# The FFN pair's fifth product: one VectorE add to the partial sum, and a GpSimd add to one result instead of two

## The chip, the core and the metric

The kernel runs on one core of one Trainium2 chip. The metric is the device time of one execution in microseconds (us). Every engine of the core has its own instruction stream and runs it in order: TensorE (PE, matrix products; PEld is its weight load, which overlaps), VectorE (DVE), ScalarE (ACT), GpSimd (POOL), and SyncE (SP), which here only issues transfers. Engines wait for each other through semaphores.

## What is computed

The reference is one transformer block with modulated layer norms, for 8 batches of 1024 rows by 256 columns, in float32. Cut to what matters:

```python
mod = (silu(c) @ wmod).reshape(8, 6, 1, 256)
sa, ca, ga, sb, cb, gb = (mod[:, i] for i in range(6))
# ga and gb are then pushed away from zero
h = layernorm(x) * (1 + ca) + sa
x = x + ga * softmax((h * w_lhs) @ (h * w_rhs).T) @ h
h = layernorm(x) * (1 + cb) + sb
x = x + gb * (relu(h @ W1 + b1) @ W2 + b2)
```

The change lies in `relu(h @ W1 + b1)`, where h has 256 columns and W1 has 1024.

## The kernel before

**Stages.** The attention of batch b runs row block by row block (8 blocks i of 128 rows). While the attention of batch b runs, the FFN of batch b-1 (the rows in two halves g of 512) is worked off beside it: steps i = 0, 1 and i = 4, 5 compute the first FFN product of a half, steps 2, 3 and 6, 7 the second. Batch 7's FFN has nothing beside it and closes the kernel. In each step PE also makes scores (`direct`, L412), turns row maxima (`max_turn`, L468), and multiplies the exponentials with the values (`product` L501, `pair_begin` L549, `pair_end` L593). DVE takes row maxima (`row_max`, L463), subtracts them (`subtract`, L475), transposes score blocks (`mirror`, L435) and closes attention blocks (`pair_out`, L608 to L621). ACT copies scores (L419) and does the exponentials (L484).

**Order.** The order of the calls in the step loop (L1150 on) is the order of the instructions on each engine: `pin` at the end ties each instruction to the one before it on its engine. So nothing overtakes anything; an instruction that comes later or takes longer moves all that stands behind it on its engine, until that engine would have idled anyway.

**The pair.** The first FFN product is made with seven half-size products instead of eight (Strassen's method in Winograd's form). For chunk c of 128 hidden columns and its partner c + 4, with the 512 rows as two halves lo and hi of 256, the seven products go to three PSUM tiles:

- `pair_products` (L728): PE writes P1 and P5 to `pa` (lo, hi), two more to `pb`, two more to `pc`. ACT copies `pa` to `kept` in SBUF (L747), so `kept[:, hi]` is the fifth product.
- `pair_sums` (L756): DVE makes the partial sum `u` = pb.lo + bias + P1 (L762), then `far` = pb.hi + bias step + u, which goes to f[c+4].hi (L765), then f[c].lo (L768), and f[c+4].lo = pc.hi + far (L771).
- `pair_last` (L773): PE writes the seventh product over `pa`.lo; DVE makes f[c].hi = pa.lo + u (L779); then one GpSimd instruction (L780) adds the fifth product to f[c].hi and f[c+4].hi together, 2 x 256 columns.
- `pair_relu` (L787): ACT applies relu to f[c] (L789) and f[c+4] (L790), 512 columns each.
- `pair_turn` (L794): GpSimd makes sums and differences of the four blocks for the second FFN product (L799 to L802).

There are 8 batches x 2 halves x 4 chunks = 64 pairs. Below they are numbered k = 0 to 63 in order: step i = 0 of batch 1 has k = 0 and 1, step 1 has 2 and 3, step 4 has 4 and 5, step 5 has 6 and 7, and batch 2 goes on with 8. k = 56 to 63 are the closing FFN.

**Buffers.** `pa`, `pb`, `pc` and most other PSUM tiles of PE (`po`, `pp`, `pq`, `pr`, and the second product's `ya` to `yd`) share a pool of four buffers, tag "a". PE's first write to a new tile waits until the last reader of the buffer's old tile is done; a buffer is given again in the order in which buffers came free. So within a step the second pair's `pb` takes the buffer that the first pair's `pb` left (last read by L765), its `pc` that of the first `pc` (last read by L771), and the tile after it (`po` or `pp`) that of the first `pa` (last read by L779). `u` and `kept` have two buffers each in SBUF.

**The step i = 4 to 5**, on DVE, in order: sums of the first pair (L762 to L771), the transposes of `y_turn` (L867) and of `mirror` (L435), L779 of the first pair, a small L277 of the next batch's norm (ACT's L281 waits for it), sums and L779 of the second pair, then the transposes of `prepare_blocks` (L322, which wait for ACT's L281), L475, L463, `pair_out` (L608 to L621), and then step 5's first pair.

Of the kernel before, what the change touches and what calls it, by code (L numbers as in the profile page):

```python
# [13 lines left out]
ALU = mybir.AluOpType  # L14
# [3 lines left out]
P = 128  # L18
# [6 lines left out]
def adaln_block_kernel(  # L25
# [13 lines left out]
    nc = tc.nc  # L39
# [7 lines left out]
    H2 = HALF // 2  # L47
    NH = NI // 2
# [673 lines left out]
    lo, hi = slice(0, H2), slice(H2, HALF)  # L722
    pairs = {}

    def mm(out, lhsT, rhs):
        nc.tensor.matmul(out, lhsT=lhsT, rhs=rhs, start=True, stop=True)  # L726
# [29 lines left out]
    def pair_sums(b, g, c):  # L756
        pa, pb, pc, kept = pairs[c]
        f = ffn["f"]
        u = work.tile([P, H2], F32, tag="u", name=f"u_{b}_{g}_{c}", bufs=2)
        pairs[c] = pa, kept, u  # L760
        far = f[:, c + NH, hi]
        nc.vector.scalar_tensor_tensor(  # L762
            u, pb[:, lo], b1_col(c), kept[:, lo], ALU.add, ALU.add
        )
        nc.vector.scalar_tensor_tensor(  # L765
            far, pb[:, hi], b1_step[:, c : c + 1], u, ALU.add, ALU.add
        )
        nc.vector.scalar_tensor_tensor(  # L768
            f[:, c, lo], pc[:, lo], b1_col(c), kept[:, lo], ALU.add, ALU.add
        )  # L770
        nc.vector.tensor_tensor(f[:, c + NH, lo], pc[:, hi], far, ALU.add)  # L771

    def pair_last(b, g, c):  # L773


        pa, kept, u = pairs.pop(c)
        f = ffn["f"]
        mm(pa[:, lo], w1s[:, 2, ts(c, P)], ffn["hT", g][0][:, 1, hi])
        nc.vector.tensor_tensor(f[:, c, hi], pa[:, lo], u, ALU.add)  # L779
        nc.gpsimd.tensor_tensor(  # L780
            f[:, c::NH, hi],
            f[:, c::NH, hi],
            kept[:, None, hi].to_broadcast([P, 2, H2]),
            ALU.add,
        )

    def pair_relu(c):  # L787
# [362 lines left out]
    for b in range(B):  # L1150
        for i in range(NT):
# [6 lines left out]
            c = i % TH * 2  # L1158
# [56 lines left out]
            if first:  # L1215
# [10 lines left out]
                if i == TH + 1:  # L1226
                    pair_relu(c - 1)
                pair_sums(fb, fg, c)
                if (b, i) == (1, 0):
                    subtract(*late)  # L1230
                if i == 4:
                    y_turn(fb, 0)
                if ahead:
                    mirror(*ahead)
                pair_last(fb, fg, c)
                if i == 0 and back:
                    for q in range(2):
# [28 lines left out]
                if sides_too:  # L1266
                    prepare_turn_apart(b + 1, 0, 0)
                middle(b, i)
                pair_sums(fb, fg, c + 1)
                pair_last(fb, fg, c + 1)  # L1270
                if i == 4:
                    if b + 1 < B:
# [105 lines left out]
    for g in range(NT // TH):  # L1378
        for c in range(NH):
            pair_products(b, g, c)  # L1380
            if g == 0 and c == 0:
                ffn_norm(b, 1)
                ffn_bias(b, 1)
            spare()
            spare()
            if c > 1:
                pair_relu(c - 2)
            if c > 0:
                pair_last(b, g, c - 1)
            pair_sums(b, g, c)  # L1390
            if g == 0 and c == 1:
                ffn_blocks(b, 1)
            elif g == 0 and c == 2:
                y_turn(b - 1, 1)
# [57 lines left out]
```

## Time and profile before

| | |
|---|---|
| median of 3 runs | 757.02 us (756.94 to 757.1) |
| the profiled execution's own time | 756.93 us |
| its span, first to last instruction | 755.1 us |
| granted TensorE clock | 1.000 |
| DVE busy | 574.9 us (76%), 1259 instructions |
| ACT busy | 374.9 us (50%), 688 instructions |
| POOL busy | 570.9 us (76%), 658 instructions |
| L780 on POOL | 64 x 1274 ns = 81.5 us |
| four DVE instructions of `pair_sums` and L779, medians | 477, 484, 475, 414 and 414 ns |

A row of the profile gives line, engine, operation, the tiles written and read (out<-in), the shapes, a count, then busy time and mean duration, and the idle time of the engine before it with what ended that. In a timeline, the first two columns are the start and the busy time in us. "POOL" is GpSimd. The duration of a DVE instruction reaches to its last write; the next one, if it waits for nothing, starts before that.

### The profile page before, as it was taken

The page shows a single profiled execution, that of the slowest core. Times are in us where ns is not written, and L with a number is a line of the kernel's source. Part 1 is how long each engine was busy: PE and PEld are TensorE (multiplying, and loading weights), DVE is VectorE, ACT ScalarE, POOL GpSimd, SP SyncE. Part 2 cuts the span into 40 slices and gives each one's busy share as a digit, 9 for nine tenths or more (in the row PEclk, how much of TensorE's full clock was granted, in tenths as well). Part 3 has the DMA queues.
Part 4 walks back from the last instruction along what each step waited for, and adds up shares of the span by engine and source line. Part 5 has one row for each costly group of instructions (what it writes and reads, how often), then busy time and mean ns, then how long its engine had stood idle before and what let it go on. Part 6 is the DMA issues. An engine that isn't in the chain of part 4 may idle for free.

```text
span 755.1 us, 11883 instructions
## 1 busy us (share of the span) xinstructions
PE 749.1 (99%) x3876; PEld 623.4 (83%) x3876; DVE 574.9 (76%) x1259; ACT 374.9 (50%) x688; POOL 570.9 (76%) x658
## 2 busy tenths in 40 slices
PE   8999999999999999999999999999999999999998
PEld 4686889788897888888888878988889788888887
DVE  7787879778796879968878688876889777685632
ACT  4554646635375454745546444563546535252521
POOL 3762796878968798788877699777996888669741
PEclk9999999999999999999999999999999999999999
DMA  9033442455443453445534555245553354133220
GB/s 308 16 112 98 131 133 74 135 178 152 127 120 123 153 153 110 147 118 158 164 99 119 153 154 161 74 127 172 155 152 85 119 166 133 50 91 126 84 85 28
DMA packets 106213, 95.21 MB, mean 126 GB/s; under 512 B 29700, under 2 KB 98848, under 8 KB 106152
## 3 DMA queue, kind: packets, MB, share of 16 engines
q1 hardware_dynamic: 98408, 85.81, 38.6%
q10 hardware_dynamic: 7744, 8.65, 3.7%
q8 instruction: 30, 0.49, 0.3%
q14 instruction: 31, 0.25, 0.1%
HBM read 50.62 MB, written 43.81 MB: 125 GB/s over the span
## 4 chain that ended last, share of the span: by engine, by line
PE 96%; DMA 1%; DVE 1%; ACT 1%; issue 0%
PE psc L412 16%; PE pa L726 11%; PE po L501 10%; PE pr L593 7%; PE pb L726 7%; PE pc L726 7%; PE yc L806 6%; PE ya L806 6%; PE yb L806 6%; PE pq L593 5%; PE pp L549 5%; PE py L916 4%; PE yd L806 3%; DMA wm<-in_L_wmod_dram 1%; PE pm L468 1%; PE pmr L194 0%
## 5 line engine op out<-in xcount | busy, mean ns | idle before, releaser
L412 PE MATMUL psc<-rT,lT 128*128 128x512 f32 (+3 forms) x384 | 134.8, 487 | 0.0
L780 POOL TENSOR_TENSOR f<-f,kept 128x512 f32<-128x512 f32 x64 | 81.5, 1274 | 42.8 <-DVE f L779 20.1
L419 ACT COPY sc<-psc 128x512 f32<-128x512 f32 (+3 forms) x96 | 44.7, 476 | 119.9 <-PE psc L412 113.0
L484 ACT ACTIVATE pT<-pT 128x1024 f32<-128x1024 f32 x64 | 67.6, 1056 | 70.6 <-DVE pT L475 70.5
L475 DVE TENSOR_TENSOR pT<-sc,pm 128x1024 f32<-128x1024 f32 x64 | 77.3, 1208 | 29.3 <-PE pm L468 13.7
L412 PEld LDWEIGHTS psc<-rT,lT 128*128 128x128 f32 x384 | 66.4, 191 | 37.2 <-issue 25.6
L501 PE MATMUL po<-xg,pT 128*128 128x257 f32 x352 | 80.6, 380 | 0.0
L463 DVE TENSOR_REDUCE m<-sc 128x1 f32<-128x1024 f32 x64 | 77.4, 1209 | 2.2 <-ACT sc L419 1.8
L501 PEld LDWEIGHTS po<-xg,pT 128*128 128x128 f32 x352 | 66.2, 190 | 10.0 <-issue 0.7
L747 ACT COPY kept<-pa 128x512 f32<-128x512 f32 x64 | 37.4, 584 | 69.3 <-PE pa L726 69.1
L726 PE MATMUL pb<-hs,w1s 128*128 128x256 f32 x256 | 65.9, 380 | 0.1
L726 PE MATMUL pc<-hT,w 128*128 128x256 f32 x256 | 65.7, 379 | 0.0
L880 POOL TENSOR_TENSOR x<-x,Y 128x512 f32<-128x512 f32 x28 | 35.1, 1276 | 29.3 <-DMA Y<-D_y 29.3
L789 ACT ACTIVATE f<-f 128x512 f32<-128x512 f32 x64 | 39.8, 622 | 34.7 <-POOL f L780 34.7
L642 POOL TENSOR_TENSOR x<-x,rows 128x256 f32<-128x256 f32 x64 | 44.8, 732 | 13.8 <-ACT rows L1022 10.6
L726 PEld LDWEIGHTS pb<-hs,w1s 128*128 128x128 f32 x256 | 48.5, 190 | 7.3 <-DVE f L765 0.8
L726 PEld LDWEIGHTS pc<-hT,w 128*128 128x128 f32 x256 | 48.6, 190 | 6.7
L806 PE MATMUL yc<-f,w2s 128*128 128x256 f32 x224 | 51.3, 379 | 0.0
L435 DVE STREAM_TRANSPOSE Tm<-sc 128x896 f32<-128x896 f32 (+6 forms) x49 | 34.3, 701 | 20.3 <-ACT sc L419 19.6
L806 PEld LDWEIGHTS yc<-f,w2s 128*128 128x128 f32 x224 | 41.5, 190 | 8.1 <-issue 2.9
L549 PEld LDWEIGHTS pp<-xg,pT 128*128 128x128 f32 x336 | 41.9, 192 | 5.1 <-DVE st_b L241 1.4
L799 POOL TENSOR_TENSOR ft<-f 128x256 f32<-128x256 f32 x56 | 40.8, 729 | 6.8 <-ACT f L790 6.8
(166 smaller groups left out, 1821.1 us busy)
## 6 DMA issues: line engine op xcount, KB each, us to landing
D_f<-T_f SPq DMA_DIRECT2D x60, 128.0 KB, 2.5
X_f<-D_f SPq DMA_DIRECT2D x15, 512.0 KB, 3.7
D_a<-T_a SPq DMA_DIRECT2D x56, 128.0 KB, 2.8
D_y<-T_y SPq DMA_DIRECT2D x56, 128.0 KB, 2.9
Y<-D_y SPq DMA_DIRECT2D x14, 512.0 KB, 3.4
out_dram<-x SPq DMA_DIRECT2D x14, 512.0 KB, 4.4
X_a<-D_a SPq DMA_DIRECT2D x13, 512.0 KB, 3.4
x<-in_L_attn_x_dram ACTq DMA_DIRECT2D x12, 512.0 KB, 3.4
```

The source lines that it names most:

```text
L412: nc.tensor.matmul(psc[:, : hi - lo], lhsT=lT_t[b, i // TH][:, k, ts(i % TH, P)], rhs=rT_t[b, n][:, k, lo - n * HALF : HALF], start=(k == ...
L419: nc.scalar.copy(score_row(b, i)[:, lo // V : hi // V, :], psc[:, : hi - lo].rearrange("p (n v) -> p n v", v=V),)
L463: nc.vector.tensor_reduce(m, score_row(b, i), AX.XY, ALU.max)
L475: nc.vector.tensor_tensor(pT.rearrange("p j (a v) -> p j a v", v=V), score_columns(b, i), pm[:, :P].rearrange("p (j a v) -> p j a v", j=1, ...
L484: nc.scalar.activation(pT_t[b, i], pT_t[b, i], AF.Exp)
L501: nc.tensor.matmul(po[:, : D + 1], lhsT=pT[:, t, :], rhs=xg_t[b][:, t, 0 : D + 1], start=(t == 0), stop=(t == NT - 1),)
L549: nc.tensor.matmul(out, lhsT=lhs[:, t, :], rhs=xg_t[b][:, h * TH + t, P : P + XS], start=(t == 0), stop=(t == TH - 1),)
L593: nc.tensor.matmul(out, lhsT=lhs[:, t, :], rhs=rhs[:, t, :], start=(t == 0), stop=(t == TH - 1),)
L642: queue.append(lambda: nc.gpsimd.tensor_tensor(out, in0, row, op))
L726: nc.tensor.matmul(out, lhsT=lhsT, rhs=rhs, start=True, stop=True)
L780: nc.gpsimd.tensor_tensor(f[:, c::NH, hi], f[:, c::NH, hi], kept[:, None, hi].to_broadcast([P, 2, H2]), ALU.add,)
L806: nc.tensor.matmul(out, lhsT=lhs(c), rhs=rhs(c), start=(c == 0), stop=(c == NH - 1))
```

## The change

`pair_sums` gets a fifth DVE instruction: after f[c+4].lo is made (L771), the fifth product is added to the partial sum in place, `u` = `kept`.hi + `u`, 128 partitions x 256 columns, both inputs in SBUF. The three uses of the old `u` and of `far` stand ahead of it. In `pair_last` L779 then puts the finished f[c].hi together (pa.lo + the new u), and the GpSimd instruction adds the fifth product to f[c+4].hi alone, 256 columns instead of 512. Otherwise no instruction changes its place on its engine.

```diff
@@ pair_sums
             f[:, c, lo], pc[:, lo], b1_col(c), kept[:, lo], ALU.add, ALU.add
         )
         nc.vector.tensor_tensor(f[:, c + NH, lo], pc[:, hi], far, ALU.add)
+        nc.vector.tensor_tensor(u, kept[:, hi], u, ALU.add)
 
     def pair_last(b, g, c):
@@ pair_last
         mm(pa[:, lo], w1s[:, 2, ts(c, P)], ffn["hT", g][0][:, 1, hi])
         nc.vector.tensor_tensor(f[:, c, hi], pa[:, lo], u, ALU.add)
         nc.gpsimd.tensor_tensor(
-            f[:, c::NH, hi],
-            f[:, c::NH, hi],
-            kept[:, None, hi].to_broadcast([P, 2, H2]),
-            ALU.add,
+            f[:, c + NH, hi], f[:, c + NH, hi], kept[:, hi], ALU.add
         )
```

## The prediction

> **What bounds the kernel now.** I read the busy totals first, then who waited for whom, then the timeline around the FFN pairs.
>
> ```profile
> PE 749.1 (99%) x3876; PEld 623.4 (83%) x3876; DVE 574.9 (76%) x1259; ACT 374.9 (50%) x688; POOL 570.9 (76%) x658
> ```
>
> ```profile
> PEld ya L806 <- POOL ft L800: 0.9, 2, 0.7
> ...
> PEld pb L726 <- DVE f L765: 0.8, 2, 0.5
> ```
>
> PE is busy for 749.1 of 755.1 us, and the rest lies mostly at the head and in the final output. Its waits for POOL and DVE once the pairs run (the second fence: the waiting engine first, then us in total, times, the longest) are two each. From the start-to-start spacing of its matmuls after 75 us I count about 1.2 us of lost PE time: 0.17 at 312.97, 0.34 at 675.11, 0.59 at 686 and crumbs. So nothing done to DVE or POOL can gain more than 1.2 us, and whatever makes PE wait is paid in full, since nothing later catches up. The question is which PE waits come near.
>
> ```profile
> 122.00:136.00 14.00, 14.00 (x88) 12.86 (x88) 13.51 (x32) 10.21 (x17) 8.55 (x9) 1.00 0.48 133
> ```
>
> This is the stretch of batch 1's steps 4 and 5 (length, then busy us of PE, PEld, DVE, ACT, POOL): DVE is busy 13.51 of 14.00 us. 76% is an average; here DVE has no room, and the added instruction stands four times in it.
>
> ```profile
> 124.03 0.42 DVE L779 TENSOR_TENSOR f<-pa,u 128x256 f32<-128x256 f32 x1
> 124.62 1.30 DVE L322 STREAM_TRANSPOSE T_a<-xg 128x512 f32<-128x512 f32 x2 [0.17 <-ACT xg L281]
> ...
> 131.22 0.48 DVE L765 SCALAR_TENSOR_TENSOR f<-pb,b_step,u 128x256 f32<-128x256 f32 x1
> ...
> 132.04 1.03 PE L726 MATMUL pb<-hs,w1s 128*128 128x256 f32 x4
> ...
> 312.97 0.73 PEld L726 LDWEIGHTS pb<-hs,w1s 128*128 128x128 f32 x4 [0.31 <-DVE f L765]
> 312.97 1.13 PE L726 MATMUL pb<-hs,w1s 128*128 128x256 f32 x4
> ```
>
> Between the second and the third row DVE idles only 0.1 us. Pair 7's pb (132.04) takes the buffer that L765 of pair 6 frees at 131.70: 0.34 us to spare. In batch 3 the same place has none left and PE loses 0.17 us: start 0.07 late, and 1.13 instead of 1.03 for the four passes.
>
> **The change, part by part.** *Removed from POOL:* 64 x (1274 - 730) ns = 34.8 us, by L780's row and L799's (128x256, median 730 ns). POOL is not what PE waits for, except at 686, where ACT's Y copy ends as late; I cost the relief at zero to -0.6 us. What hides it is PE's own work; POOL's results have several us to spare elsewhere.
>
> *Added to DVE:* 64 adds of 128x256 with both inputs in SBUF. Alone, such an add took 406 ns (L997, 8 partitions), and the next instruction starts 0.33 us after it (L771 at 123.70 to L779 at 124.03). So +0.33 us where other DVE work stands between L771 and L779; where L779 comes next it must wait for the finished u: 0.41 + 0.03 = +0.44. That is 21 to 28 us of DVE time in all, if the add runs unhindered.
>
> *Whether it runs unhindered* is the second cost:
>
> ```profile
> L621 DVE SCALAR_TENSOR_TENSOR x<-W,rl,x x21: 340/483/1355, 109.9 to 696.9; 128x128 f32<-128x128 f32 x21
> ...
> L277 DVE SCALAR_TENSOR_TENSOR rs<-mva,ra x14: 139/174/1270, 38.9 to 574.7; 128x4 f32<-128x4 f32 x14
> ...
> L609 DVE TENSOR_TENSOR W<-pr,W x21: 423/424/427, 107.9 to 694.9; 128x256 f32<-128x256 f32 x21
> ...
> 284.21 1.27 POOL L576 TENSOR_TENSOR pT<-s,pT 128x512 f32<-128x512 f32 x1
> 284.23 1.27 DVE L277 SCALAR_TENSOR_TENSOR rs<-mva,ra 128x4 f32<-128x4 f32 x1
> ```
>
> Minimum, median, maximum in ns. L621 on W and L277 read two SBUF tensors, and their times spread by 1 us: a 128x4 instruction that takes 139 ns lasted 1270 when it started 0.02 us behind a POOL instruction of 1.27 us. L609, which reads PSUM and one SBUF tensor, never varies, though POOL runs beside it too. So a DVE instruction with two SBUF inputs waits for the POOL instruction under way; from these rows (1355 against 340, with 1.2 us of POOL left) the wait is POOL's remainder less about 0.2 us. All five pair instructions of before read PSUM and one SBUF tensor and are immune; the added one is not. Taking POOL's row at 0.33 us behind each L771 start, POOL is at work at 39 of 64, with 24.1 us left in all; less 0.2 each that is about 16 us. Bounds: 0 (POOL always idle there) and 64 x 1.27 = 81 us; I take 16, on top of the 21 to 28.
>
> The Trainium skill (SBUF — State Buffer, "Who interferes with whom") has the rule: a DVE instruction with two SBUF inputs contends with a GpSimd instruction that reads SBUF, and the later one fully blocks. L277's row agrees. By a reading without that rule the 16 us would be nil.
>
> *What of this reaches PE*, place by place. A wait of PE for L765 costs its lateness against PE's due start plus 0.16 us for the weight load that was not ahead (312.97: L765 ends 0.01 after the due start, 0.17 lost; 675.11: 0.19 after, 0.34 lost).
>
> 1. Step 5 of batches 1, 2, 4, 5, 6, all with 0.34 to spare. POOL is idle at both adds of step 4, so they cost 0.33 + 0.44 = 0.77. The idle before L322 and the overlap of starts take back 0.26 (L322 may start 0.33 behind L779's start, at 124.36, and started at 124.62): 0.51 stays until L765 of pair 6. Late by 0.51 - 0.34 = 0.17, cost 0.33; five times, 1.65 us.
> 2. Batch 3's step 5: POOL's L577 holds the add of step 4 by 0.4, so 0.9 arrives where 0.17 is already lost; a 0.46 us DVE gap without a visible cause at 309.68 may or may not stay. Then the add of pair 6 meets the y_add L880, and L779 frees po's buffer late. 0.4 to 1.4, I take 0.9.
> 3. Batch 1's step 0: the add stands ahead of L475, whose exponential ends 0.09 before PE's product needs it. 0.3.
> 4. Batch 7's steps 5 to 7: DVE waits for PE at 669.74 and 670.63, which absorbs step 4; but the adds of pairs 54 and 55 (+0.44 each, and 0.4 each behind POOL's L880 and L801; 0.25 comes back at L655, which no longer meets a long L780) bring L463 to 682.1 where PE needs it at 681.6, and ACT's exponential before the Y copy late too. 0.85.
> 5. Elsewhere (steps 0 and 1, closing FFN) DVE idles 1 to 2 us between (before L322 at 175.72, before L779 at 731.59) and this covers the adds; without that cover each would cost 0.3 to 0.5. 0.1 for a tight pc at 710.
>
> SP's transfers behind L867 and L322 go out 0.3 to 0.5 later; their reader, ACT's L342, has 5 us until PE needs its tiles. POOL's L780 stands in the same place but now waits only for L771, not L779; relu of f[c] no longer waits for POOL.
>
> Sum: 1.65 + 0.9 + 0.3 + 0.85 + 0.1 = 3.8 us. The profiled execution took 756.93 (span 755.1), 0.09 under the median of 757.02, so the forecast is 757.0 + 3.8 = **760.8 us**.
>
> **Rivals.**
> *A, DVE absorbs it (same):* if the add issues quicker or POOL's relief lets ACT's L281 and DVE's L655 run earlier, the lateness in place 1 falls under 0.34 and only places 3 and 4 stay in part: 757.0 + 0.5 to 1.4, say 758.0. For it: DVE is 76% busy, and L655 (143 to 1084 ns) now often waits for L780. Against: 13.51 of 14.00.
> *B, POOL's relief decides (not slower):* L780 was waited for by ACT 34.7 us in 24 relus; if that chain, and not DVE's, sets the Y copy and the ft sums at 686, PE gets back up to 0.59 there, and 0.5 at the L765 waits if DVE is spared its waits for POOL too: 755.9 to 757.0, say 756.3. It decides from the point where DVE's lateness stays under 0.3 everywhere. Against: at 686 ACT waits for DVE's L475 (2.14 us), not for POOL.
> *C, the port waits pile up (much slower):* in steps 4 and 5 four adds at 0.44 plus 0.4 of port wait make 3.4; with 0.6 absorbed, 2.8 a batch reach po, x 7 = 20 us at worst; a third of that gives 764 to 766. For it: L880 runs 2.5 us at a stretch just there. Against: po has 1.2 us to spare behind L779.
>
> **How the numbers follow.** A measurement of this kernel tells about 0.2% (1.5 us) from no change: below 755.5, above 758.5. Forecast 0.70 (758.6 to 763.0, its own range), A 0.12, B 0.07, C 0.11. The range must leave out 0.2 at most: 757.2 (A's and half of B's edge) to 764.5 (the lower part of C). Slower: forecast and C, 0.81; faster: the low end of B, 0.03; same: the rest, 0.16.
>
> **What would show it.** The added row on DVE: minimum near 410 ns, maximum above 1 us where POOL was under way (right), or all within 20 ns (the port cost is wrong). L780 at 730 ns. PEld pb waiting for L765 in seven places instead of two, some 0.3 to 0.5 us of idle each. PE's busy time unchanged, DVE's up by 30 to 45 us, POOL's down by 30 to 35. Wrong if PE shows no new waits at 132, 222, 404, 494 and 584 us, or if the new waits are mostly for ACT or DMA.

## The result, and the profile after

The changed kernel takes **761.71 us** (median of 4 runs, 760.98 to 762.68) against 757.06 us for the one before (4 runs, 756.94 to 758.32): ratio 1.0058, 95% interval 1.0041 to 1.0076. The profiled execution took 761.94 us with a span of 760.1 us, 5.0 us over the span before, at a granted clock of 1.000 in both. The added instruction is line 772 now, so L779, L780 and L880 of before are L780, L781 and L878 after.

The busy totals of after come first (us, share of the span, instructions), then the added row in the answer for the tile `u` (minimum, median, maximum in ns, first and last start) and POOL's halved addition among the costliest groups (busy us, mean ns, then idle time before it).

```profile
PE 752.4 (99%) x3876; PEld 621.8 (82%) x3876; DVE 614.1 (81%) x1323; ACT 376.8 (50%) x688; POOL 543.5 (71%) x658
```

```profile
L772 DVE TENSOR_TENSOR u<-kept,u x64: 414/418/1448, 78.4 to 744.6; 128x256 f32<-128x256 f32 x64
```

```profile
L781 POOL TENSOR_TENSOR f<-f,kept 128x256 f32<-128x256 f32 x64 | 50.5, 789 | 53.0 <-DVE f L771 50.4
```

DVE is busy 39.2 us more, POOL 27.4 us less. The 64 additions take 40.7 us in all; at their minimum of 0.414 us they would take 26.5, so 14.2 us of it is waiting for POOL, as the maximum of 1448 ns shows (27 of the 64 take over 450 ns). POOL's halved addition takes 789 ns on average and not the 730 of its like-sized rows: it is let go by L771, starts within L772 and is held in its turn. In `e1_pool_half` below, which has no addition on DVE, it has a median of 728 and a maximum of 753 ns.

What PE waits for is in the list of waits of after (the waiting engine, what released it, us in total, times, the longest):

```profile
PEld pb L726 <- DVE f L765: 2.6, 7, 0.5
PEld pc L726 <- DVE pr L611: 2.2, 6, 0.5
PEld ya L804 <- POOL f L800: 1.0, 1, 1.0
PEld pm L468 <- DVE m L463: 1.0, 2, 0.8
...
PE ya L804 <- ACT Y L816: 0.7, 1, 0.7
...
PE pr L593 <- DVE rs L277: 0.5, 1, 0.5
...
PEld po L501 <- DVE f L780: 0.4, 1, 0.4
```

The wait of pb for L765 stood twice before and stands seven times now; the wait of pc for L611, six times, is new. To see what they cost I compared the start of every matmul in the two traces, one by one: PE runs the same 3876 in the same order, so where the difference of the starts jumps, there time was lost. The jumps by the prediction's places, in us:

| place | forecast | trace |
|---|---|---|
| 1: step 5 of batches 1, 2, 4, 5, 6 | 1.65 | 2.09 |
| 2: batch 3, steps 4 and 5 | 0.9 | 1.15 |
| 3: batch 1, step 0 | 0.3 | 0.41 |
| 4: batch 7, steps 5 to 7 | 0.85 | 1.41 |
| 5: elsewhere | 0.1 | 0.06 |
| small shifts | - | -0.1 |
| sum | 3.8 | 5.0 |

Place 1, batch 1, in the timeline of before (start us, busy us, engine, line), and then of after (in brackets the idle time and what ended it):

```profile
128.92 0.30 DVE L611 TENSOR_TENSOR pr<-W,pq 128x128 f32<-128x128 f32 x1
...
129.77 1.03 PE L726 MATMUL pc<-hT,w 128*128 128x256 f32 x4
```

```profile
129.88 0.29 DVE L611 TENSOR_TENSOR pr<-W,pq 128x128 f32<-128x128 f32 x1
130.22 0.73 PEld L726 LDWEIGHTS pc<-hT,w 128*128 128x128 f32 x4 [0.34 <-DVE pr L611]
130.22 1.13 PE L726 MATMUL pc<-hT,w 128*128 128x256 f32 x4
...
132.17 0.48 DVE L765 SCALAR_TENSOR_TENSOR f<-pb,b_step,u 128x256 f32<-128x256 f32 x1
132.71 0.73 PEld L726 LDWEIGHTS pb<-hs,w1s 128*128 128x128 f32 x4 [0.35 <-DVE f L765]
132.71 1.13 PE L726 MATMUL pb<-hs,w1s 128*128 128x256 f32 x4
```

DVE's lateness is met at two handovers. Pair 6's pc takes the buffer of the old `pq`, which L611 of `pair_out` reads last; it starts 0.10 late, and the four passes take 1.13 for 1.03, since the next weight load was not ahead: 0.21. That uses up part of the lateness, and pb two us later meets the rest: 0.11 late and again 0.10. Together 0.42 in each of five batches.

The second stall does not add to the bill. Counted from where PE stands ahead of pc, L765 comes 0.60 later than in the trace before, and pb alone, with its 0.34 to spare and 0.16 for the weight load, would have cost 0.60 - 0.34 + 0.16 = 0.42 too: what PE loses at pc, pb no longer has to wait for. I looked at these five batches in all seven traces whose kernels have the additions of step 4 (after, e2, e3, e4, e7, e8, e9 below): the lateness of L765 runs from 0.59 to 1.61, and PE's loss at pc and pb together is 0.18 less every time.

The 0.60 itself begins at the second addition of step 4:

```profile
124.72 0.42 DVE L772 TENSOR_TENSOR u<-kept,u 128x256 f32<-128x256 f32 x1
...
125.24 0.42 DVE L780 TENSOR_TENSOR f<-pa,u 128x256 f32<-128x256 f32 x1
```

```profile
L780 DVEq EVENT_SEMAPHORE  x64: 21/21/21, 78.9 to 745.1; - x64
```

L780 has to wait for two engines now, for PE's seventh product and for DVE's own `u`, and one of the waits has become an instruction of its own in DVE's queue (second fence). L780 starts 0.10 us behind the end of the addition, in 36 of the 41 pairs in which it directly follows; in the other five it waits for PE. In the trace before, L765, which waits for `u` alone, starts 0.035 behind L762; L609, which has such a second wait, starts at least 0.10 behind L608.

Places 2 and 4 come from additions that met POOL at work. Batch 3 and then batch 7, timeline of after:

```profile
302.43 1.27 POOL L577 TENSOR_TENSOR pT<-pT 128x512 f32<-128x512 f32 x1
302.66 1.32 DVE L772 TENSOR_TENSOR u<-kept,u 128x256 f32<-128x256 f32 x1
...
305.32 0.38 DVE L780 TENSOR_TENSOR f<-pa,u 128x256 f32<-128x256 f32 x1
```

```profile
677.73 2.50 POOL L878 TENSOR_TENSOR x<-x,Y 128x512 f32<-128x512 f32 x2 [3.10 <-DMA Y<-D_y]
...
679.22 1.30 DVE L772 TENSOR_TENSOR u<-kept,u 128x256 f32<-128x256 f32 x1
...
686.30 0.32 PE L468 MATMUL pm<-ident,m 128*128 128x128 f32 x1 [0.57 <-DVE m L463]
```

In batch 3 the addition starts 0.23 behind L577 and lasts 1.32, so L577 held it 0.9; L780 of the same pair ends at 305.70, and `pr`, which by the order of the buffers takes the one that L780 reads last, starts 0.67 late (the profile puts this wait down to L277, which is next on DVE and ends at 305.76). In batch 7 the second of the two L878 is under way; po, pm and ya then start late one after the other (0.31, 0.79 and 0.32), pm because L463 comes too late.

### The profile page after: what moved, and what is told of

It is laid out like the page before. It is cut to its first block, busy times and chain, and to the rows that moved or that the text cites. A ratio compares the mean times of both kernels' runs of the same rounds, so it can differ in the third digit from the quotient of the medians.

```text
span 760.1 us, 12022 instructions
## 1 busy us (share of the span) xinstructions
PE 752.4 (99%) x3876; PEld 621.8 (82%) x3876; DVE 614.1 (81%) x1323; ACT 376.8 (50%) x688; POOL 543.5 (71%) x658
## 4 chain that ended last, share of the span: by engine, by line
PE 95%; DVE 3%; DMA 1%; issue 0%; ACT 0%; DVEq 0%
PE psc L412 16%; PE pa L726 10%; PE po L501 10%; PE pr L593 7%; PE pb L726 7%; PE pc L726 7%; PE ya L804 6%; PE yc L804 6%; PE yb L804 6%; PE pp L549 5%; PE pq L593 5%; PE py L914 4%; PE yd L804 3%; DMA wm<-in_L_wmod_dram 1%; PE pm L468 1%; PE pmr L194 0%
## 5 line engine op out<-in xcount | busy, mean ns | idle before, releaser
L475 DVE TENSOR_TENSOR pT<-sc,pm 128x1024 f32<-128x1024 f32 x64 | 77.3, 1207 | 18.4 <-DMA sc<-D_m 9.3
L781 POOL TENSOR_TENSOR f<-f,kept 128x256 f32<-128x256 f32 x64 | 50.5, 789 | 53.0 <-DVE f L771 50.4
L463 DVE TENSOR_REDUCE m<-sc 128x1 f32<-128x1024 f32 x64 | 77.4, 1210 | 2.4 <-ACT sc L419 1.8
L878 POOL TENSOR_TENSOR x<-x,Y 128x512 f32<-128x512 f32 x28 | 35.8, 1301 | 31.3 <-DMA Y<-D_y 26.9
L435 DVE STREAM_TRANSPOSE Tm<-sc 128x896 f32<-128x896 f32 (+6 forms) x49 | 34.3, 699 | 19.6 <-ACT sc L419 19.6
```

The lines of the kernel that those rows point to most:

```text
L463: nc.vector.tensor_reduce(m, score_row(b, i), AX.XY, ALU.max)
L475: nc.vector.tensor_tensor(pT.rearrange("p j (a v) -> p j a v", v=V), score_columns(b, i), pm[:, :P].rearrange("p (j a v) -> p j a v", j=1, ...
L781: nc.gpsimd.tensor_tensor(f[:, c + NH, hi], f[:, c + NH, hi], kept[:, hi], ALU.add)
```

## Experiments

Each was timed beside the kernel before on the same chip: 757.55 us (15 runs) for the first four, 757.47 (17) for the next four, 757.42 (16) for the last two. Ratios are to that, with their 95% intervals. My theory: the loss is DVE's lateness in steps 4 and 5, made of the added instruction's own time and of its waits for POOL, paid where little was to spare. The rivals: POOL's relief matters too; each addition costs the same wherever it stands.

**The two halves of the change apart.** `e1_pool_half` is the diff's second part alone (f[c].hi then gets no fifth product), `e2_add_only` its first part alone, with GpSimd still adding to both results.

```diff
@@ e1_pool_half, against before
         nc.gpsimd.tensor_tensor(
-            f[:, c::NH, hi],
-            f[:, c::NH, hi],
-            kept[:, None, hi].to_broadcast([P, 2, H2]),
-            ALU.add,
+            f[:, c + NH, hi], f[:, c + NH, hi], kept[:, hi], ALU.add
         )
@@ e2_add_only, against before
         nc.vector.tensor_tensor(f[:, c + NH, lo], pc[:, hi], far, ALU.add)
+        nc.vector.tensor_tensor(u, kept[:, hi], u, ALU.add)
```

> GpSimd's add halved, the DVE add left out, so the fifth product is missing from f[c].hi. Theory (all of the loss is DVE's: the added instruction and its wait for POOL make DVE late at PE's buffers): no loss, 756.0 to 757.2 us, and at most 1.2 us of gain because PE waits no longer than that before. Rival (the halved GpSimd instruction itself, which now ends at other times, makes the loss): 759 or more.

> The DVE add stays, GpSimd adds to both results as before, so f[c].hi has the fifth product twice. Theory: at least the whole loss, 761.5 to 766 us, since POOL's instructions are long again and the add waits for their remainder; place 1 (batches 1, 2, 4, 5, 6 at step 5, 0.42 us each in the changed kernel) unchanged, because POOL idles at the adds of step 4. Rival (the loss comes from both halves together): below 760.

Measured: e1 757.14 us (11 runs), 0.9998 (0.9989 to 1.0007): the relief alone is worth nothing that these runs can tell. e2 **771.92 us** (4 runs), 1.0198 (1.0184 to 1.0212), above every expectation; place 1 stays at 0.41 to 0.42 a batch, as expected. The parts don't add: 0 and +14.4 make +4.65 together. The waits of e2, then its timeline in batch 1's step 2:

```profile
PEld ya L807 <- ACT f L790: 9.3, 7, 1.7
PE ya L807 <- ACT f L790: 6.4, 7, 1.3
```

```profile
94.65 1.18 DVE L772 TENSOR_TENSOR u<-kept,u 128x256 f32<-128x256 f32 x1
...
95.93 0.42 DVE L780 TENSOR_TENSOR f<-pa,u 128x256 f32<-128x256 f32 x1
...
96.44 1.27 POOL L781 TENSOR_TENSOR f<-f,kept 128x512 f32<-128x512 f32 x1 [0.89 <-DVE f L780]
97.74 0.63 ACT L790 ACTIVATE f<-f 128x512 f32<-128x512 f32 x1 [2.50 <-POOL f L781]
98.42 0.70 PE L807 MATMUL ya<-f,w 128*128 128x256 f32 x2 [0.67 <-ACT f L790]
```

A late L780 holds POOL's long addition, this holds relu, and relu holds the second product in step 2 of all seven batches: 0.9 to 1.5 us each, 8.3 of the 10.1 us by which e2's span exceeds that of after. In the changed kernel POOL's addition waits only for L771, and relu of f[c] only for L780. So GpSimd's half of the change gains nothing by itself, and saves some 10 us once VectorE has the addition.

**The wait for POOL.** Both move the addition to directly ahead of L780 (line 779 there); e3 takes the fifth product from SBUF, e4 from PSUM, so that it has one SBUF input.

```diff
@@ e3_late_sbuf, against after
-        nc.vector.tensor_tensor(u, kept[:, hi], u, ALU.add)
...
         mm(pa[:, lo], w1s[:, 2, ts(c, P)], ffn["hT", g][0][:, 1, hi])
+        nc.vector.tensor_tensor(u, kept[:, hi], u, ALU.add)
         nc.vector.tensor_tensor(f[:, c, hi], pa[:, lo], u, ALU.add)
@@ e4_late_psum, against e3_late_sbuf
-        nc.vector.tensor_tensor(u, kept[:, hi], u, ALU.add)
+        nc.vector.tensor_tensor(u, pa[:, hi], u, ALU.add)
```

> As the changed kernel, but the add stands directly ahead of L780's add to f[c].hi instead of behind the sums (control of the next one). Theory: the same occupancy and the same two SBUF inputs, so 760.5 to 763 us. Rival (the place in line is what costs, because it stands ahead of the score transposes and of L475): below 759.5.

> As the control, but the fifth product is read from PSUM (pa.hi) and not from kept, so the add has one SBUF input. Theory: its duration is 410 to 430 ns everywhere, no more waits for POOL; places 2, 3 and 4 (2.97 us in the changed kernel) shrink to 0.6 to 1.3, place 1 (2.09 us, occupancy alone) stays: 759.5 to 760.5 us, 1 to 2 us below the control. Rival (the waits for POOL cost nothing, occupancy is all): the control's time within 0.4. Rival (the waits for POOL are all): 757 to 758.

Measured: e3 763.90 us (4 runs), 1.0092 (1.0078 to 1.0106), 0.9 above its range; e4 760.73 us (5 runs), 1.0042 (1.0029 to 1.0056), 0.2 above its range and 3.2 below e3 where 1 to 2 were expected. The rivals miss by more. The added rows of e3 and e4, and e3's timeline in batch 1:

```profile
L779 DVE TENSOR_TENSOR u<-kept,u x64: 380/559/1486, 80.0 to 748.6; 128x256 f32<-128x256 f32 x64
```

```profile
L779 DVE TENSOR_TENSOR u<-pa,u x64: 382/412/425, 80.4 to 744.0; 128x256 f32<-128x256 f32 x64
```

```profile
133.11 2.68 POOL L878 TENSOR_TENSOR x<-x,Y 128x512 f32<-128x512 f32 x2 [3.72 <-DMA Y<-D_y]
133.25 1.41 DVE L779 TENSOR_TENSOR u<-kept,u 128x256 f32<-128x256 f32 x1
```

With one SBUF input the times spread by 43 ns, with two by 1.1 us, at the same place beside the same POOL work. The pair bounds the wait for POOL: at most 3.2 us of e3's 6.4; the other 3.2 us is DVE's own time, which e4 pays too, mostly in places 1, 3 and 4. Not all of the 3.2 is that wait. In e4 L780 has only the wait for `u` left and starts 0.03 behind the addition, in e3 0.10; at step 4 of the batches of place 1, where no addition meets POOL in either, e3 still loses 0.55 a batch and e4 0.47, which makes 0.4 us. The Trainium skill (SBUF — State Buffer, "Who interferes with whom") says that the order of issue, not the shape, decides who blocks; the runs agree. In e3 the addition starts 0.14 behind L878 and lasts 1.41; in after, at the same pair, it starts at 133.29, ahead of L878 (134.07), and lasts 0.42.

**The same place, from PSUM.** `e5_same_psum` should have split the loss of the change itself.

```diff
@@ against after
-        nc.vector.tensor_tensor(u, kept[:, hi], u, ALU.add)
+        nc.vector.tensor_tensor(u, pa[:, hi], u, ALU.add)
```

> The change with one operand replaced: the added instruction stays behind L771, but takes the fifth product from PSUM (pa.hi) instead of its copy in SBUF, so it has one SBUF input. Theory (occupancy of DVE plus waits for the POOL instruction under way): every added instruction takes 0.38 to 0.43 us, the stalls at 81 (0.41) and at pc and pb of batches 1, 2, 4, 5, 6 (0.42 each) stay, those of batch 3 (1.15) and batch 7 (1.41) fall to 0.3 and 0.6: 5.0 - 1.7 = 3.3 us over before, 760.3 to 761.2 us. Rival 1 (the wait for POOL is hidden in this place and cost something only directly ahead of L780): as the change, 761.5 to 762.3. Rival 2 (the wait for POOL is most of the loss): 757.5 to 759.

Measured: **865.3 us** (6 runs), 1.1442 (1.1411 to 1.1473): all three expectations missed. The added row, and the timeline at the first pairs:

```profile
L772 DVE TENSOR_TENSOR u<-pa,u x64: 411/413/416, 78.8 to 848.2; 128x256 f32<-128x256 f32 x64
```

```profile
83.46 0.41 DVE L772 TENSOR_TENSOR u<-pa,u 128x256 f32<-128x256 f32 x1
...
84.02 0.67 PE L726 MATMUL pa<-hT,w1s 128*128 128x256 f32 x2 [1.34 <-DVE u L772]
```

The row itself is immune to POOL, as expected. But PE's seventh product writes the other half of the same tile `pa`, and it now waits until DVE has read: 62 stalls, most of 1.5 to 1.6 us, 107 us together by the matmul starts. (The profiled run took 869.79 us, at a granted clock of 0.990.) So it tells nothing of the share of POOL in this place. Whether the chip needs that wait, or only the program's bookkeeping by tile, the trace doesn't say.

**Where it is paid.** The change in the rows of one half alone; the other 32 pairs as before. (In these and the last two kernels the added line is 773 and the y_add 882.)

```diff
@@ e6_first_half, against after
-        nc.vector.tensor_tensor(u, kept[:, hi], u, ALU.add)
+        if g == 0:
+            nc.vector.tensor_tensor(u, kept[:, hi], u, ALU.add)
...
             f[:, c + NH, hi], f[:, c + NH, hi], kept[:, hi], ALU.add
+        ) if g == 0 else nc.gpsimd.tensor_tensor(
+            f[:, c::NH, hi], f[:, c::NH, hi],
+            kept[:, None, hi].to_broadcast([P, 2, H2]), ALU.add,
         )
@@ e7_second_half, against e6_first_half
-        if g == 0:
+        if g == 1:
...
-        ) if g == 0 else nc.gpsimd.tensor_tensor(
+        ) if g == 1 else nc.gpsimd.tensor_tensor(
```

> The change in the rows of half g = 0 alone (steps 0 and 1 of each batch, and the first half of the closing FFN); the 32 pairs of g = 1 as before. Theory (only places with little to spare pay): the stall of 0.41 at 81 us, 0.1 elsewhere: 0.3 to 0.8 us over before, 757.8 to 758.4. Rival (each added instruction pays about the same, 5.0 / 64 = 0.08 us): half of the loss, 759.5 to 760.5.

> The change in the rows of half g = 1 alone (steps 4 and 5, second half of the closing FFN). Theory: the stalls of batches 1 to 7 in steps 4 to 7 all stay, 2.1 + 1.1 + 1.4 = 4.6 us over before, 761.6 to 762.4; PEld pb waits for L765 seven times as with the change. Rival (each instruction pays the same): 759.5 to 760.5.

Measured: e6 758.24 us (11 runs), 1.0011 (1.0002 to 1.0019): half of the additions for under a fifth of the loss, 0.42 of it at 81 us, as the theory had it. e7 760.67 us (5 runs), 1.0045 (1.0033 to 1.0058): between theory and rival, and in neither range. By the matmul starts place 1 is there unchanged (0.42 in each of batches 1, 2, 4, 5, 6), but batch 3 loses 0.24 for 1.15 and batch 7 0.54 for 1.41. Batch 7 in the timeline of e7:

```profile
676.62 2.80 POOL L882 TENSOR_TENSOR x<-x,Y 128x512 f32<-128x512 f32 x2 [3.33 <-DMA Y<-D_y]
...
677.88 0.42 DVE L773 TENSOR_TENSOR u<-kept,u 128x256 f32<-128x256 f32 x1
```

Here the addition starts 1.26 us behind the first L882, just as that ends, takes 0.42 and holds the second one (2.80 us for the two, 2.50 in after; the second alone, from 677.85, takes 1.57 for 1.27). In after it started 1.49 us behind L878 and found the second under way. L882 waits for a transfer; a shift of 0.23 us between that transfer and DVE goes with a difference of almost 0.9 us of PE. In e10 below the addition meets L882 again, and batch 7 loses 1.25. In batch 3 e7's addition starts at 302.24, 0.5 us after L577 (1.27 us from 300.48) is over. So places 2 and 4 are no fixed price.

**Twice the dose.** A second addition, overwritten later.

```diff
@@ against after
         nc.vector.tensor_tensor(u, kept[:, hi], u, ALU.add)
+        nc.vector.tensor_tensor(f[:, c, hi], kept[:, hi], u, ALU.add)
```

> The change with a second addition behind the first, of the same shape and inputs, into f[c].hi, which L780 overwrites afterwards; the output stays the same. Theory (a reserve of 0.34 us in steps 4 and 5 that the first instruction has used up): each further 0.33 there is paid in full, 4 x 0.33 x 7 batches = 9 us, plus 0.4 where POOL is under way: 768 to 774 us, the loss more than doubled. Rival (the loss grows with the number of instructions, without a reserve): twice the loss, 765.5 to 767. Rival (the wait for the unfinished u, not DVE's occupancy, makes the loss): hardly more than the change, 762 to 764.

Measured: **805.47 us** (4 runs), 1.0638 (1.0624 to 1.0651), far above all three. The two rows of e8:

```profile
L772 DVE TENSOR_TENSOR u<-kept,u x64: 412/416/1424, 78.3 to 788.3; 128x256 f32<-128x256 f32 x64
```

```profile
L773 DVE TENSOR_TENSOR f<-kept,u x64: 426/833/1382, 79.0 to 788.8; 128x256 f32<-128x256 f32 x64
```

The second addition has a median of 833 ns, twice the first: POOL's addition is let go by L771, starts within the first, and so stands in the way of the second nearly every time. DVE's busy time grows by 52.2 us over after, the span by 43.1. The expectation had only added 0.33 us in steps 4 and 5; it forgot that the change's own POOL instruction starts right there. Nor do the stalls keep to steps 4 and 5: 7.8 us of the 43.1 are step 2's second product waiting for relu, in all seven batches, the chain that e2 had opened. The direction holds (the first addition uses up the reserve, 43.1 of the further 52.2 us are paid), the size was wrong by a factor of three and more.

**Which additions make the stalls of step 5.** The condition `g == 1 and c < 2` (the pairs of step 4) and `g == 1 and c >= 2` (those of step 5), each with two pairs of the closing FFN; otherwise as e7.

> The change in the first two of the four pairs of half g = 1 alone (steps 4 of batches 1 to 7, and c = 0, 1 of the second half of the closing FFN), all other pairs as before. Theory (the two added instructions of step 4 make the lateness that PE meets a step later, at pc and pb of step 5): those stalls stay with 5 x 0.42 = 2.1 us, batches 3 and 7 add 0.1 to 1.2: 2.2 to 3.3 us over before, 759.6 to 760.9 us. Rival (a pair pays for its own addition): the stalls of step 5 go, 757.4 to 758.6.

> The change in the last two pairs of half g = 1 alone (steps 5 of batches 1 to 7, and c = 2, 3 of the second half of the closing FFN). Theory: the additions of step 5 stand behind the L765 and L611 that PE waits for there, so no stall at pc and pb in batches 1, 2, 4, 5, 6; what stays is batch 7 (0.3 to 1.4, by whether the addition meets L882 under way) and up to 0.3 in batch 3: 757.8 to 759.1 us. Rival (a pair pays for its own addition): 759.6 to 760.9.

Measured: e9 759.81 us (6 runs), 1.0030 (1.0019 to 1.0042); e10 758.70 us (11 runs), 1.0017 (1.0008 to 1.0026). Waits of e9, then of e10:

```profile
PEld pb L726 <- DVE f L765: 2.6, 7, 0.5
PEld pc L726 <- DVE pr L611: 2.0, 6, 0.3
```

```profile
PEld pb L726 <- DVE f L765: 0.5, 1, 0.5
```

With the additions of step 4 alone, pc and pb of step 5 stall as with the whole change: 0.42 in each of the five batches, 2.1 us. With those of step 5 alone the wait of pc for L611 is gone, that of pb is left once, and the five batches lose nothing there; what is left is batch 7 (1.2 us, its addition met L882 and lasted 1.13) and pieces of up to 0.4. Both theories hold within their ranges. The rival, that a pair pays for its own addition, falls.

## Why the prediction was right

- **The bound.** "Nothing done to DVE or POOL can gain more than 1.2 us, and whatever makes PE wait is paid in full": the jumps of PE's starts add up to the 5.0 us of the span, none is won back, and e1 shows no gain.
- **POOL's relief at zero to -0.6.** e1: nothing. The reason given (several us to spare for POOL's results) holds only as long as L780 is on time; e2 shows the chain through relu that opens otherwise. The forecast said that relu of f[c] no longer waits for POOL, but set no price on it; that this keeps the chain shut it didn't see.
- **The added row.** Forecast 0.41 and up to over 1 us with some 16 us of waits; trace 0.414 to 1.448 with 14.2. The sum is near partly by luck: 39 additions were to meet POOL, for 0.4 us each, and 27 took over 0.45, some 0.5 longer each.
- **Place 1, term mis-sized: 1.65, measured 2.09.** The chain was right (additions of step 4, lateness at step 5; e9 and e10), and so was the price, lateness less 0.34 to spare plus 0.16. The lateness was 0.60 and not 0.51: +0.44 for the second addition of step 4 let L780 start 0.03 behind the finished u, and it starts 0.10 behind it, at 125.24 (+0.52). The 0.33 of the first and the 0.26 won back before L322 came as said. The forecast also left out pc of pair 6, which takes the buffer of `pq` (L611 ends at 130.17, 0.05 behind the due start of pc; L765 at 132.65, 0.05 behind that of pb); this splits the 0.42 into two stalls and does not raise it.
- **Place 3, 0.3, measured 0.41.** By the way forecast: PE's product at 81.25 waits for ACT's exponential, which waits for L475; the addition ahead of that takes 0.56.
- **Place 2, 0.9, measured 1.15, by another way.** The forecast had the lateness arrive at pb and po; it arrived already in step 4, at `pr`, which takes L780's buffer, and L577 held the addition 0.9 where 0.4 was said. Place 4, 0.85, measured 1.41: here the port wait of pair 54 was put at 0.4 and was 0.9. e7 shows that both sizes hang on what POOL has under way when the addition starts; in batch 7 0.23 us made the difference. e3 and e4 put the part of such waits at 2.8 us or less of 6.4 at the later place; at the change's own place the split stays open, since e5 changed another wait.
- **Rivals.** A (DVE absorbs it) fails at the five new stalls; B (the relief decides) at e1; C named the right thing, waits that pile up, but only those of batches 3 and 7 can be followed to PE.
- **What would show it.** DVE's busy time up by 39.2 (30 to 45 said), pb waiting seven times, new waits at the five places: as said. POOL went down by 27.4 and not 30 to 35, L781 takes 789 ns and not 730, since DVE holds it (without the addition, in e1, POOL goes down by 34.3). PE's busy time was to stay and rose by 3.3: part of each stall falls inside a group of passes (1.13 us for 1.03) and counts as busy; the rest I didn't follow.

## What to carry to other kernels

On engines that work in program order, the price of an added instruction is the lateness that is left at a later handover, less what that handover has to spare: list every buffer that the delayed instructions free, not only the nearest. A lateness that is met at two handovers in a row was paid once here, by the tighter of the two. Count also what the instruction behind the added one has to wait for: L780 with its second wait started 0.07 us later each time, and that is most of what the forecast of place 1 missed. Moving work from one engine to another is one change and not two: the relief here gained nothing and yet spared 10 us, because it cut a wait that the added work would have lengthened. An addition on VectorE with both inputs in SBUF is priced by what GpSimd does at that moment; taking an input from PSUM avoids it, unless the matmul that comes next still has to write the same tile.

## What the runs showed of the hardware

The wait between VectorE and GpSimd goes both ways: POOL's 128x256 addition takes 730 ns unhindered, and took 0.92 us at 680.18 in after, where it started within a waiting L772. A matmul into one half of a PSUM tile waited 1.3 us for a read of the other half (e5), whoever asks for that wait. A DVE instruction that waits for PE and for the DVE instruction just ahead of it starts 0.10 us behind that one's end (L780 in after and e3), one that waits for the latter alone 0.03 (L780 in e4). And one transfer moves by itself: the one that ACT's L342 waits for in batch 6 let it start at 590.81 in the trace before and at 591.51 in e1's, whose matmuls stood otherwise alike but for 0.5 us at the head and 0.1 at 139.8, and PE lost 1.0 us there: a difference of 1 us between the spans of two single traces is no evidence until it is followed to the wait that made it.
